# Shared threshold rows and a split of the column sums between GpSimd and VectorE, in a fused convolution and wavelet kernel

## The chip, the cores and the metric

The kernel runs on one core of a Trainium2 chip. The metric is the device time of one execution in microseconds (us). The core has five engines that this text names: TensorE (matmuls, "PE" in the profile, with its weight loads "PEld"), VectorE ("DVE"), ScalarE ("ACT"), GpSimd ("POOL") and SyncE ("SP"), which issues all the transfers of this kernel. Each engine works through its own list of instructions in the order in which the program gives them; semaphores make an instruction wait for one on another engine.

## The reference

The input x has 4 images of 64 channels of 256 x 256 float32 values. Four layers follow each other.

Layers 0, 2 and 3 are long convolutions. A small network with sines makes a filter along rows and one along columns for each channel; their outer product is convolved with the image (in the reference by FFT), and `x * bias` is added. Because the filter is an outer product, the kernel multiplies with a Toeplitz matrix along rows and with another along columns.

Layer 1 is a wavelet layer:

```python
f1 = haar2d(x)
for i in range(2):
    f3 = f1 * v[i]
    f4 = jnp.einsum('bchw,oc->bohw', f3, conv_w[i])
    f5 = jnp.sign(f4) * relu(jnp.abs(f4) - tau[i])
    acc = acc + f5
y = haar2d(acc, inverse=True) + x
```

The Haar transform along one axis takes sums and differences of neighbours, then again of the sums, for eight levels. `tau` is the threshold: one 256 x 256 map for each of the two branches, the same for all channels and images.

## The kernel before

**Phases.** Phase A does layer 0 and the forward Haar transform and stores coefficients in DRAM. Phase B multiplies by v, mixes channels with matmuls, takes the threshold (`less`, L680, and `threshold`, L685) and stores the mixed coefficients. Phase C does the inverse transform and layers 2 and 3. The images form two groups; phase B of the first group runs beside the second half of phase A, and phase B of the second group beside phase C.

**Phase A.** It has 64 rounds (`total`, L462), each of two channels of two images, and each round has ten pieces (`piece`, L524). In pieces 0 to 3 of round t TensorE does the rows of round t (`rows`), in pieces 4 and 5 the second half of the Haar transform of round t-3 as matmuls (`product`), and in pieces 6 to 9 the columns of round t-1 (`columns`). The PSUM results are put away one piece later (`flush`): after two column pieces VectorE makes two residuals, `x * bias + ps` (`residual`, L503), so a round has four of them, two in piece 8 and two in piece 0 of the next round. They fill the tile `x1`.

**The forward column sums.** `forward_free` (L362) does the first half of the Haar transform, along the free axis of `x1`. For half = 128, 64, 32, 16, 8, 4, 2, 1 it takes the differences (into the tile `fw`) and the sums (into a tile `h<half>`, which has one buffer and is the input of the next level) of neighbours. An instruction of level `half` writes 8 x half elements for each of 128 partitions: 1024, 512, 256, 128, 64, 32, 16, 8. It is a generator: each step issues one instruction, 16 in all, on GpSimd. The steps for round t-2 are taken in round t (L535 and L536): three in each of pieces 0 to 3, two in each of pieces 4 and 5. `x1` and `fw` have two buffers.

**The thresholds.** Before phase B, `scale_thresholds` (L313) loads `tau` into SBUF and multiplies it with a factor for each level. `put_thresholds` (L321) then copies it to DRAM, 64 times, one copy for each channel, because a step of phase B needs 128 partitions (64 channels x 2 rows) that all hold the same two rows. This takes 64 transfers of 512 KB. The DRAM rows are padded by 128 elements. `load_v` (L588) reads the copies back for each step of phase B, 64 steps for each group.

**The order of work.** `beside` (L1002) merges two lists of pieces. Up to piece 4 + 4 of round 34 it merges phase A with `rest` (L303): the networks of the other two layers, the copies of their filters, and the threshold writes, spread evenly (`merged`, L298). After that it merges phase A with phase B of the first group, whose units (`piece`, L722) have three pieces each: in the first VectorE multiplies (L663) and GpSimd adds (L703 to L707), in the second VectorE subtracts and applies the threshold (L683, L688) and TensorE mixes (L644). All transfers go through SyncE in program order.

Of the kernel before, what the change touches and what calls it, by code (L numbers as in the profile page):

```python
# [41 lines left out]
F32 = mybir.dt.float32  # L42
AF = mybir.ActivationFunctionType
ALU = mybir.AluOpType
# [3 lines left out]
P = 128  # L48
B, C, N = 4, 64, 256
# [9 lines left out]
ITEMS = 3  # L59
SPAN = ITEMS * PERIOD  # L60
REPEATS = 12
COPIES = 2 * REPEATS * ITEMS

FIRST = 4
# [35 lines left out]
def conv_haar_kernel(  # L100
# [13 lines left out]
    coef = [coefficients(f"coef{g}") for g in range(GROUPS)]  # L114
    mixed = [coefficients(f"mixed{g}") for g in range(GROUPS)]
    unshrunk = coefficients("unshrunk")
    thresholds = dram.tile([STEPS, 2, C, 2 * W + PAD], F32, tag="thresholds", name="thresholds")
    filt = [dram.tile([ROUNDS, 2, REPEATS, ITEMS, PERIOD], F32, tag=f"filt{l}", name=f"filt{l}") for l in range(NL)]

    def pool(name, bufs, stack=ctx, **kw):  # L120
# [174 lines left out]
    def half(r):  # L295
        return slice(r * ROW, (r + 1) * ROW)
# [16 lines left out]
    def scale_thresholds():  # L313

        per_level_sb = mp.tile([P, N], F32, tag="per_level", name="per_level_sb")
        nc.sync.dma_start(per_level_sb, per_level.partition_broadcast(P))
        nc.sync.dma_start(tau_sb.rearrange("p r w -> p (r w)"), tau)
        rows = tau_sb.rearrange("p r (h k) -> p (r h) k", k=N)
        nc.vector.tensor_tensor(rows, rows, per_level_sb.unsqueeze(1).to_broadcast([P, 4, N]), ALU.mult)

    def put_thresholds(copies, r, i):  # L321

        of = tau_sb[half(i), r].unsqueeze(1).to_broadcast([ROW, copies.stop - copies.start, W])
        nc.sync.dma_start(thresholds[:, r, copies, i * W : (i + 1) * W], of)

    puts = [(slice(n, n + 4), r, i) for n in range(0, C, 4) for r in range(2) for i in range(2)]
    rest = merged(rest, [scale_thresholds] + [lambda at=at: put_thresholds(*at) for at in puts])

    TILES = [(r, c) for r in range(2) for c in range(2)]

# [31 lines left out]
    def forward_free(src, dst, name):  # L362

        cur, half = src, HALF
        whole = dst.rearrange("p n (k q) -> p n k q", k=BLOCKS)
        to = dst.rearrange("p n (k q) -> p (n k) q", k=BLOCKS)
        while half > 0:
            sums = nxt = None
            if half > 1:
                nxt = ac.tile([P, 2 * M, half], F32, tag=f"h{half}", name=f"{name}{half}", bufs=1)  # L370
                sums = nxt
            else:
                sums = whole[:, :, 0:1, 0]
            if half < BLOCKS:
                pair = cur.rearrange("p n (t q) -> p n t q", q=2)
                diffs = whole[:, :, half : 2 * half, 0]
            else:
                m = half // BLOCKS
                pair = cur.rearrange("p n (k t q) -> p (n k) t q", k=BLOCKS, q=2)
                diffs = to[:, :, m : 2 * m]  # L380
                sums = sums.rearrange("p n (k t) -> p (n k) t", k=BLOCKS)
            even, odd = pair[:, :, :, 0], pair[:, :, :, 1]
            nc.gpsimd.tensor_tensor(diffs, even, odd, ALU.subtract)  # L383
            yield
            nc.gpsimd.tensor_tensor(sums, even, odd, ALU.add)
            yield
            cur = nxt
            half //= 2
# [70 lines left out]
    def phase_a():  # L459


        total = GROUPS * ROUNDS  # L462
        st = [dict() for _ in range(total)]

        def filters(t):
            if t < total:
                st[t]["toep"] = first_toep[t] if t < len(first_toep) else load_toeplitz(0, t)

        def load(t):
            if t < total:  # L470
                st[t]["x"] = first_x[t] if t < len(first_x) else load_x(t)

        def rows(t, j):
            s = st[t]
            if j == 0:
                s["y"] = big("t0", f"ay_{t}", 2)
            if j % 2 == 0:
                s["ps"] = banks(f"a1ps{j}_{t}")
            toeplitz(s["ps"], blocks(s["x"]), filters_x(s["toep"]), j)
            if j % 2:  # L480
                for r, ps in enumerate(s["ps"]):
                    y = blocks(s["y"])[:, r, j - 1 : j + 1]
                    later(lambda y=y, ps=ps: nc.scalar.copy(y, ps))  # L483

        def columns(t, j):
            s = st[t]
            if j == 0:
                s["x1"] = big("m0", f"x1_{t}", 2)
            if j % 2 == 0:
                s["ps2"] = banks(f"a2ps{j}_{t}")  # L490
            toeplitz(s["ps2"], blocks(s["y"]), filters_y(s["toep"]), j)
            if j % 2:
                for e, ps in enumerate(s["ps2"]):
                    later(lambda e=e, ps=ps: residual(t, e, j, ps))
            if j == BLOCKS - 1:
                s["fw"] = big("m1", f"fw_{t}", 2)
                s["ops"] = forward_free(s["x1"], s["fw"], f"f{t}_")

        def residual(t, e, j, ps):
            s = st[t]  # L500
            c = t % ROUNDS * CI + e
            to, old = (blocks(s[name])[:, e, j - 1 : j + 1] for name in ("x1", "x"))
            nc.vector.scalar_tensor_tensor(to, old, bias_sb[:, c : c + 1], ps, ALU.mult, ALU.add)  # L503

        def product(t, bp):
            s = st[t]
            if bp == 0:

                s["f"] = big("out", f"f_{t}", 2)
            two = banks(f"a3ps{bp}_{t}")  # L510
            fw = blocks(s["fw"])
            haar(two, lambda r, c: fw[half(r), c, 2 * bp : 2 * bp + 2], forward_sb)
            for b, ps in enumerate(two):
                f = s["f"][:, 4 * bp + 2 * b : 4 * bp + 2 * b + 2]
                later(lambda f=f, ps=ps: nc.scalar.copy(f, ps))  # L515

        def store(t):
            for to, f in all_rows(coef[t // ROUNDS], t % ROUNDS, st[t]["f"], t >= ROUNDS):
                nc.sync.dma_start(to, f)
            st[t].clear()  # L520

        middle = BLOCKS + 2

        def piece(t, j):  # L524
            flush()
            if t == 0 and j == 0:
                filters(0)
                filters(1)
                load(0)
                load(1)  # L530
            if j == 1 and t < 2:
                copies[t]()
            if j == 2:
                filters(t + 2)
            if j < middle and 1 < t:  # L535
                run(st[t - 2]["ops"], 3 if j < BLOCKS else 2)  # L536
            if j < BLOCKS:
                if t < total:
                    rows(t, j)
            elif j < middle:  # L540
                if 2 < t:
                    product(t - 3, j - BLOCKS)
            elif 0 < t <= total:
                columns(t - 1, j - middle)
            if j == middle + 1 and t > 2:
                store(t - 3)
            if j == A_PIECES - 1:
                load(t + 2)

        copies = spread(0, FIRST, ROUNDS, 2)  # L550
        pieces = [lambda t=t, j=j: piece(t, j) for t in range(total) for j in range(A_PIECES)]

        last = [lambda: [piece(total, j) for j in range(BLOCKS + 1)]]
        last += [lambda j=j: piece(total, j) for j in range(BLOCKS + 1, A_PIECES)]
        last += [lambda bp=bp: (flush(), product(total - 2, bp)) for bp in range(2)]
        t = total - 1
        end = [lambda: (flush(), run(st[t]["ops"], 16), store(t - 1))]
        end += [lambda bp=bp: (flush(), product(t, bp)) for bp in range(2)]
        end.append(lambda: (flush(), store(t)))
        return pieces, last, end  # L560

    def phase_b(grp):
# [25 lines left out]
        def load_v(s):  # L588
            if s >= STEPS:
                return  # L590
            d = st[s]
            d["v"], d["tau"] = [], []

            def fetch(first, count, tag):
                t = bp.tile([P, 2, count, W], F32, tag=tag, name=f"{tag}_{grp}_{first}_{s}", bufs=3)
                at = slice(first * W, (first + count) * W)
                nc.sync.dma_start(t[:, 0].rearrange("p i w -> p (i w)"), v[s, :, at])
                nc.sync.dma_start(t[:, 1].rearrange("p i w -> p (i w)"), thresholds[s].rearrange("r c w -> (r c) w")[:, at])
                d["v"] += [t[:, 0, i] for i in range(count)]
                d["tau"] += [t[:, 1, i] for i in range(count)]  # L600

            fetch(0, 2 if grp < GROUPS - 1 else 1, "v")
            if grp == GROUPS - 1 and not raw(2 * s + 1):
                fetch(1, 1, "raw")
# [564 lines left out]
```

## Time and profile before

| What | Value |
|---|---|
| Median of 3 runs | 2643.49 us (2638.67 to 2643.73) |
| The profiled execution | 2637.55 us, its span 2635.8 us |
| TensorE matmuls busy | 2323.6 us, 88% |
| VectorE busy | 1692.5 us, 64% |
| ScalarE busy | 1450.0 us, 55% |
| GpSimd busy | 2075.0 us, 79% |
| Transfers | 713.20 MB, 78.5% of the 16 DMA engines' time for the main queue |

The span is the time from the first to the last instruction. A row of the groups names the source line, the engine, the operation, output and inputs by their names in the program, the shape and the count; then the busy time in us and the mean of one in ns; then the idle time of the engine ahead of it and what ended that. The waits name who waited for whom, with the total in us, the number of times and the longest. A line number L383 is line 383 of the kernel before.

### The profile page before, as it was taken

To read this page: it belongs to the slowest core of one execution; us is meant where nothing else is said; L and a number is where in the kernel's file an instruction comes from. 1 tells how busy PE (TensorE), PEld (TensorE's weight loads), DVE (VectorE), ACT (ScalarE), POOL (GpSimd) and SP (SyncE) were. 2 spreads that over 40 slices of the span, in tenths; PEclk is the share of its full clock that TensorE was granted. 3 is DMA by queue.
4 is the path that set the end of the run, shared out by engine and by line. 5 is a ranking of instruction groups with operands and counts; after the bars stand their busy time and mean duration, and the time that the engine had idled before them with its cause. 6 is when DMAs were issued, how large, how long until landed. Compare 5 with 4: busy or idle time off the path is not lost.

```text
span 2635.8 us, 119315 instructions
## 1 busy us (share of the span) xinstructions
PE 2323.6 (88%) x53298; PEld 1950.2 (74%) x53298; DVE 1692.5 (64%) x1815; ACT 1450.0 (55%) x2446; POOL 2075.0 (79%) x2428
## 2 busy tenths in 40 slices
PE   6988788867777777788799999999989999999999
PEld 4778777745455444565578777777779999999999
DVE  4321112277887888975676777777757777777763
ACT  1333232256766777745566666666656555555652
POOL 1776666688888999987877777767879999999991
PEclk8999899988998999988899999999999999999999
DMA  6888898869989999975798889889966666666653
GB/s 190 273 278 282 267 276 273 300 227 341 317 305 330 330 346 347 346 251 186 261 324 316 316 310 332 319 311 316 331 218 223 213 212 214 219 214 212 219 169 111
DMA packets 238073, 713.20 MB, mean 271 GB/s; under 512 B 32238, under 2 KB 33583, under 8 KB 233336
## 3 DMA queue, kind: packets, MB, share of 16 engines
q1 hardware_dynamic: 237560, 705.57, 78.5%
q8 instruction: 419, 6.86, 1.1%
q14 instruction: 94, 0.77, 0.1%
HBM read 428.16 MB, written 277.28 MB: 268 GB/s over the span
## 4 chain that ended last, share of the span: by engine, by line
PE 41%; DVE 4%; DMA 3%; ACT 2%; issue 2%; POOL 1%; SPq 1%; DVEq 0%; ACTq 0%; POOLq 0%
PE c2c L335 9%; PE c2r L335 9%; PE c1r L335 8%; PE c1c L335 8%; PE c0ps L347 4%; PE f L644 3%; DVE cy L919 1%; DVE m L688 1%; DMA toep<-filt 1%; DMA g<-mixed 1%; DVE x L683 1%; DVE x L663 1%; ACT g L401 0%; POOL i L424 0%; ACT x L678 0%
## 5 line engine op out<-in xcount | busy, mean ns | idle before, releaser
L424 POOL TENSOR_TENSOR i<-i,g 128x16 f32<-128x16 f32 x744 | 438.5, 610 | 27.2
L335 PEld LDWEIGHTS a2ps<-toep,ay 64*64 64x64 f32 x8192 | 343.4, 140 | 126.6 <-ACT f L515 84.4
L644 PE MATMUL f<-ft,mix 64*64 64x512 f32 x2048 | 313.3, 632 | 123.4 <-DVE x L663 104.7
L335 PE MATMUL a1ps<-toep,x 64*64 64x256 f32 (+3 forms) x8192 | 353.9, 313 | 67.1 <-DMA x<-in_x 48.0
L335 PEld LDWEIGHTS a1ps<-toep,x 64*64 64x64 f32 x8192 | 316.5, 141 | 129.2 <-issue 70.1
L335 PE MATMUL a2ps<-toep,ay 64*64 64x128 f32 (+3 forms) x8192 | 360.9, 312 | 51.5 <-ACT f L515 50.8
L503 DVE SCALAR_TENSOR_TENSOR x<-x,bias_sb,a2ps 128x512 f32<-128x512 f32 x256 | 179.4, 742 | 337.8 <-issue 148.1
L335 PEld LDWEIGHTS c2c<-toep,ch 64*64 64x64 f32 x8192 | 306.5, 134 | 48.0 <-issue 24.7
L335 PEld LDWEIGHTS c1c<-toep,ch 64*64 64x64 f32 x8192 | 308.1, 134 | 42.4 <-issue 19.0
L483 ACT COPY ay<-a1ps 128x512 f32<-128x512 f32 x256 | 137.3, 589 | 365.2 <-PE a1ps L335 364.6
L335 PEld LDWEIGHTS c1r<-toep,z 64*64 64x64 f32 x8192 | 300.0, 135 | 28.9 <-issue 13.4
L424 POOL TENSOR_TENSOR ci<-i,g 128x1024 f32<-128x1024 f32 x124 | 316.6, 2574 | 4.5
L335 PE MATMUL c1r<-toep,z 64*64 64x64 f32 (+3 forms) x8192 | 316.0, 299 | 3.5 <-ACT z L888 1.8
L335 PEld LDWEIGHTS c2r<-toep,cy 64*64 64x64 f32 x8192 | 296.5, 134 | 29.8 <-issue 19.1
L335 PE MATMUL c2c<-toep,ch 64*64 64x128 f32 (+3 forms) x8192 | 311.6, 298 | 6.3 <-issue 3.5
L335 PE MATMUL c2r<-toep,cy 64*64 64x192 f32 (+3 forms) x8192 | 313.8, 298 | 3.2 <-issue 3.2
L335 PE MATMUL c1c<-toep,ch 64*64 64x128 f32 (+3 forms) x8192 | 311.6, 298 | 5.1 <-ACT ch L900 2.6
L706 POOL TENSOR_TENSOR gt<-m,ft 128x512 f32<-128x512 f32 x128 | 163.4, 1277 | 179.7 <-DVE m L688 179.7
L900 ACT COPY ch<-c2r 128x512 f32<-128x512 f32 x256 | 137.3, 590 | 281.8 <-PE c2r L335 281.1
L669 ACT ACTIVATE m<-x 128x1024 f32<-128x1024 f32 x194 | 206.3, 1063 | 144.7 <-DVE x L663 108.1
L383 POOL TENSOR_TENSOR fw<-x 128x1024 f32<-128x1024 f32 x64 | 121.7, 1902 | 189.9 <-DVE x L503 187.6
L663 DVE TENSOR_TENSOR x<-f,v 128x1024 f32<-128x1024 f32 x192 | 233.6, 1216 | 57.1 <-PE f L644 56.5
(85 smaller groups left out, 3983.6 us busy)
## 6 DMA issues: line engine op xcount, KB each, us to landing
toep<-filt SPq DMA_DIRECT2D x768, 112.0 KB
ft<-coef SPq DMA_DIRECT2D x128, 512.0 KB
mixed<-gt SPq DMA_DIRECT2D x128, 512.0 KB
g<-mixed SPq DMA_DIRECT2D x256, 256.0 KB
x<-in_x SPq DMA_DIRECT2D x128, 256.0 KB
thresholds<-tau_sb SPq DMA_DIRECT2D x64, 512.0 KB
coef<-f SPq DMA_DIRECT2D x128, 256.0 KB
x<-in_x SPq DMA_DIRECT2D x32, 1024.0 KB
```

The costliest lines, as they stand in the source:

```text
L335: nc.tensor.matmul(ps[r][half(c), j % 2, k * ROW :], data[half(r), c, k, bass.ts(j, ROW)], t(r, c)[:, : N - k * ROW], start=k == 0, stop=k ...
L347: nc.tensor.matmul(ps[r][half(c)].rearrange("p h k -> p (h k)"), matrix[half(r)], pairs(r, c).rearrange("p h k -> p (h k)"), start=True, s ...
L383: nc.gpsimd.tensor_tensor(diffs, even, odd, ALU.subtract)
L424: engine.tensor_tensor(to, s, d, op)
L483: later(lambda y=y, ps=ps: nc.scalar.copy(y, ps))
L503: nc.vector.scalar_tensor_tensor(to, old, bias_sb[:, c : c + 1], ps, ALU.mult, ALU.add)
L644: nc.tensor.matmul(un[u]["f4"][half(q), b, :], mixers[0][half(r), bass.ts(i, C)], st[s]["f"][half(r), b], start=True, stop=True, tile_posi ...
L663: nc.vector.tensor_tensor(un[u]["x"], un[u]["f4"], both(u, "v"), ALU.mult)
L669: nc.scalar.activation(un[u]["m"], un[u]["x"], AF.Sign)
L683: nc.vector.tensor_tensor(un[u]["a"], un[u]["a"], both(u, "tau"), ALU.subtract)
L706: nc.gpsimd.tensor_tensor(g[:, 0], m[:, 0], st[s]["f"][:, 0], ALU.add)
L900: later(lambda y=y, ps=ps: nc.scalar.copy(y, ps))
```

## The change

There are two edits.

**Thresholds.** The DRAM tile holds 16 copies of each row (`SHARED`) in place of 64. They are written by eight transfers, each with two copies of the whole scaled `tau` from all 128 partitions (1 MB), in place of 64 transfers of 512 KB. A load for phase B reads each copy into four neighbouring partitions; the number and the size of the loads stay. The layout of `tau` in SBUF changes with it (host side). Since the list of pieces is shorter, the multiplication moves from the first place of `rest` to one eighteenth of its length.

**Column sums.** The levels half = 8, 4, 2 and 1 (`COARSE`), eight instructions of 64, 32, 16 and 8 elements for each partition, are issued on VectorE in place of GpSimd. The steps are taken two in each of pieces 0 to 3 (the fine levels, on GpSimd) and two in each of pieces 6 to 9 (the coarse ones, on VectorE), none in pieces 4 and 5. They come after the piece's `flush`, so after the residuals in piece 8.

```diff
+SHARED = 16
+COARSE = 8
...
-    thresholds = dram.tile([STEPS, 2, C, 2 * W + PAD], F32, tag="thresholds", name="thresholds")
+    thresholds = dram.tile([STEPS, 2, SHARED, 2 * W + PAD], F32, tag="thresholds", name="thresholds")
...
-    def put_thresholds(copies, r, i):
-
-        of = tau_sb[half(i), r].unsqueeze(1).to_broadcast([ROW, copies.stop - copies.start, W])
-        nc.sync.dma_start(thresholds[:, r, copies, i * W : (i + 1) * W], of)
-
-    puts = [(slice(n, n + 4), r, i) for n in range(0, C, 4) for r in range(2) for i in range(2)]
-    rest = merged(rest, [scale_thresholds] + [lambda at=at: put_thresholds(*at) for at in puts])
+    def put_thresholds(copies):
+
+        n = copies.stop - copies.start
+        of = tau_sb.rearrange("p i w -> p (i w)").unsqueeze(1).to_broadcast([P, n, 2 * W])
+        nc.sync.dma_start(thresholds.rearrange("s r c w -> (s r) c w")[:, copies, : 2 * W], of)
+
+    rest = merged(rest, [scale_thresholds] + [lambda n=n: put_thresholds(slice(n, n + 2)) for n in range(0, SHARED, 2)])
...
-            nc.gpsimd.tensor_tensor(diffs, even, odd, ALU.subtract)
+            engine = nc.gpsimd if half > COARSE else nc.vector
+            engine.tensor_tensor(diffs, even, odd, ALU.subtract)
             yield
-            nc.gpsimd.tensor_tensor(sums, even, odd, ALU.add)
+            engine.tensor_tensor(sums, even, odd, ALU.add)
             yield
...
-            if j < middle and 1 < t:
-                run(st[t - 2]["ops"], 3 if j < BLOCKS else 2)
+            if not BLOCKS <= j < middle and 1 < t:
+                run(st[t - 2]["ops"], 2)
...
-                nc.sync.dma_start(t[:, 1].rearrange("p i w -> p (i w)"), thresholds[s].rearrange("r c w -> (r c) w")[:, at])
+                of = thresholds[s].rearrange("r c w -> (r c) w")[:, at].unsqueeze(1).to_broadcast([2 * SHARED, C // SHARED, count * W])
+                nc.sync.dma_start(t[:, 1].rearrange("p i w -> p (i w)"), of)
...
-        "tau": f(by_row("tau").transpose(2, 0, 1, 3).reshape(P, 2 * W)),
+        "tau": f(by_row("tau").reshape(P, 2 * W)),
```

More of the change, by code (lines that the diff above doesn't have):

```diff
@@ L316, in scale_thresholds @@
         nc.sync.dma_start(per_level_sb, per_level.partition_broadcast(P))
-        nc.sync.dma_start(tau_sb.rearrange("p r w -> p (r w)"), tau)
-        rows = tau_sb.rearrange("p r (h k) -> p (r h) k", k=N)
+        nc.sync.dma_start(tau_sb.rearrange("p i w -> p (i w)"), tau)
+        rows = tau_sb.rearrange("p i (h k) -> p (i h) k", k=N)
         nc.vector.tensor_tensor(rows, rows, per_level_sb.unsqueeze(1).to_broadcast([P, 4, N]), ALU.mult)
-    def put_thresholds(copies, r, i):
-        of = tau_sb[half(i), r].unsqueeze(1).to_broadcast([ROW, copies.stop - copies.start, W])
-        nc.sync.dma_start(thresholds[:, r, copies, i * W : (i + 1) * W], of)
-    puts = [(slice(n, n + 4), r, i) for n in range(0, C, 4) for r in range(2) for i in range(2)]
-    rest = merged(rest, [scale_thresholds] + [lambda at=at: put_thresholds(*at) for at in puts])
+    def put_thresholds(copies):
[3 more added lines that the diff above has]
+    rest = merged(rest, [scale_thresholds] + [lambda n=n: put_thresholds(slice(n, n + 2)) for n in range(0, SHARED, 2)])
     TILES = [(r, c) for r in range(2) for c in range(2)]
```

## The prediction

> **What bounds the kernel now.** The first view is the time by stage. Its columns: stretch in us, its length, then busy us and instruction count of TensorE (matmuls, weight loads), VectorE, ScalarE and GpSimd, the granted clock, the share of the 16 DMA engines, GB/s.
>
> ```profile
> 169.40:509.10 339.70, 287.21 (x6572) 262.75 (x6576) 67.49 (x96) 98.69 (x192) 227.27 (x385) 0.93 0.87 275
> ...
> 612.50:859.50 247.00, 186.87 (x3124) 128.61 (x3120) 204.68 (x191) 171.56 (x231) 213.80 (x235) 0.92 0.92 318
> 859.50:1132.20 272.70, 213.05 (x3748) 138.24 (x3744) 244.38 (x229) 206.69 (x277) 257.06 (x283) 0.97 0.96 340
> ```
>
> Row one is phase A beside the threshold writes ("stage 1"): VectorE idles for 80% of it, the transfers are at 87%. The others are phase A beside phase B's first group ("stage 2"): VectorE 83 and 90%, GpSimd 87 and 94%. From 1290 us on neither half of the change has work except the threshold reads.
>
> The waits of the first 600 us (total, times, longest):
>
> ```profile
> POOL fw L383 <- DVE x L503: 182.5, 33, 52.4
> ...
> PE a1ps L335 <- DMA x<-in_x: 48.0, 34, 3.5
> ```
>
> TensorE is late for the x loads, about once a round; GpSimd has time to spare. A round's length comes from the starts of the 1024-element column-sum pairs (L383): 54.4, 169.4 after nine rounds, 509.1 after 24 more, so 12.8 and 14.15 us. Single rounds of 10.4 us occur, so TensorE can do that.
>
> The groups by shape give the prices (busy us, mean ns):
>
> ```profile
> L383 POOL TENSOR_TENSOR fw<-x 128x1024 f32<-128x1024 f32 x64 | 121.7, 1902 | 189.9 <-DVE x L503 187.6 <-issue 2.2
> ...
> L383 POOL TENSOR_TENSOR fw<-f 128x64 f32<-128x64 f32 x64 | 18.8, 294 | 5.0
> ```
>
> The timelines (start, us) show how a round's parts follow each other in stage 1, and what a small VectorE operation meets while GpSimd runs:
>
> ```profile
> 320.47 1.41 DVE L503 SCALAR_TENSOR_TENSOR x<-x,bias_sb,a2ps 128x512 f32<-128x512 f32 x2 [0.72 <-PE a2ps L335]
> ```
>
> ```profile
> 321.96 1.89 POOL L383 TENSOR_TENSOR fw<-x 128x1024 f32<-128x1024 f32 x1 [0.69 <-DVE x L503]
> ```
>
> ```profile
> 1163.48 1.89 POOL L385 TENSOR_TENSOR f<-x 128x1024 f32<-128x1024 f32 x1
> 1163.64 1.84 DVE L426 SCALAR_TENSOR_TENSOR i_x<-g 128x8 f32<-128x8 f32 x2 [2.27 <-DMA g<-mixed]
> ```
>
> GpSimd's chain for a round starts 0.08 us after its last residual pair. The two 8-element operations at 1163.64 take 1.84 us: they end when the GpSimd operation does (1165.37), plus 0.1. Elsewhere the line takes 160 to 168 ns.
>
> A stage 2 round (residuals end at 927.6; its GpSimd chain starts there):
>
> ```profile
> 937.45 0.41 POOL L385 TENSOR_TENSOR f<-f 128x128 f32<-128x128 f32 x1
> ...
> 940.16 1.23 DVE L683 TENSOR_TENSOR a<-a,v 128x1024 f32<-128x1024 f32 x1 [1.06 <-ACT a L678]
> ...
> 943.77 1.40 DVE L503 SCALAR_TENSOR_TENSOR x<-x,bias_sb,a2ps 128x512 f32<-128x512 f32 x2
> ...
> 948.70 1.40 DVE L503 SCALAR_TENSOR_TENSOR x<-x,bias_sb,a2ps 128x512 f32<-128x512 f32 x2
> ```
>
> Level 16 is done at +10.3 us; VectorE stands still until +12.6 at piece 6; residuals at +16.2 and +21.1; the round ends at +22.5.
>
> [...] here the granted clock is 0.92 from 612 to 859 us and 0.97 after, and the rows don't show what starts the low spells. [...]
>
> **The threshold writes.** 64 issues of 512 KB (33.5 MB) become 8 of 1 MB (8.4 MB). Stage 1 moves 275 GB/s at 87%, so 316 at 100%: 25.2 MB less is 80 us of all 16 engines, 2.4 us a round over 33 rounds. SyncE saves 56 issues of 628 ns (median), 35 us or 1 us a round, off the path. Transfers then need about 12.2 - 2.4 = 9.8 us a round, TensorE 10.4. The reads keep count and size, but four neighbouring partitions read one row. The trace has no such pair to compare; 130 reads carry some 50 MB, 150 us of transfers at 340 GB/s, and 5% either way bounds it at ±7 us. I take 0: the Toeplitz loads also read shared copies. The multiplication of the thresholds moves from the start to after piece 0 of round 2. Two loads go before it on SyncE's queue, behind x; its VectorE wait (22.6 us now, at the start) has some 7 us of cover, while GpSimd sums round 0. If that cover were gone it would cost once, under 10 us.
>
> **The coarse levels in stage 1.** Eight GpSimd operations leave: 294+298+251+250+228+228+222+208 = 1.98 us. VectorE gains eight. [...] Two of one level overlap by about 0.08 us as those of L426 do, so the levels cost 0.40, 0.33, 0.29, 0.27 with their dependences, 1.3 us.
>
> The order matters more. Program order on VectorE in round t is: residuals of t-2 (piece 0), coarse 8 and 4 of t-2 (pieces 6, 7), residuals of t-1 (piece 8), coarse 2, coarse 1, residuals of t-1 (next piece 0). Coarse 8 waits for GpSimd's fine levels of t-2; behind it stand the residuals of t-1, and GpSimd's fine levels of t-1 wait for those. So a round holds one closed loop: fine levels 2(1.90+1.05+0.61+0.40) = 7.95, handing over 0.08, coarse 1.3, residuals 2 x 1.41, handing over 0.08: 12.25 us. GpSimd is idle during the VectorE part[...]. TensorE waits for banks that the residuals release, but has 1.9 us of room. The loop is longer than TensorE's 10.4 and the transfers' 9.8, and is the new bound: 12.3 to 12.6. Against 14.15 that is 24 x 1.7 = 40 us less; in the first nine rounds (12.8) the networks' VectorE work sits in the same queue, and I take no gain. Stage 1: **-40**.
>
> **The coarse levels in stage 2.** The merge puts 404 phase B pieces over 270 of phase A (L1002), so a round of ten holds five units of three. New GpSimd order: fine 128 and 64, add, fine 32 and 16, add, add. Level 16 still ends at +10.3. VectorE reaches piece 6 at +11.5 and idles to +12.6; GpSimd is then in an add (1.28 or 2.37 us each), so coarse 8 goes at its end, +11.7 to +12.75: delay 0 to 0.35. Coarse 4 at +15.1 waits for an add that ends near +15.3: 0.45 with its own time. Coarse 2 (+18.1) and coarse 1 (+20.9) find GpSimd between adds: 0.29 and 0.27. Sum 1.0 to 1.4 a round; 12 rounds x 1.2 = 14. In the ten rounds of 612 to 859 VectorE waits 2 to 4 us a round for TensorE at piece 7 (28.8 us for L663 in the waits of 600 to 850), which covers coarse 8 and 4: 10 x 0.6 = 6. Four opening rounds: 2. If the cover is gone, 0.7 more each. What is behind these waits: phase B's subtractions, then ScalarE's magnitudes and TensorE's mixing. GpSimd's 2 us less is worth nothing while VectorE leads. Stage 2: **+22**. Bounds: -10 (GpSimd's load was half the limit) and +80[...].
>
> **The end of phase A.** The last round's sums run in one stretch: 9.9 us on GpSimd become 8.0 + 1.4, but the coarse waits hold phase C's first residuals, which already wait 7.2 us for the same chain. **+3**.
>
> Sum: -40 + 22 + 3 = -15 from the profiled 2637.55 (span 2635.8 and 1.75 around it): 2622. The median, 2643.49, lies 5.9 higher: **2628**.
>
> **Rivals.**
> 1. [...] Each coarse pair in stage 2 that finds GpSimd entering an add first pays 1.28 or 2.37 more, 1.65 on average. For: the second of two 64-element operations of L426 lost its turn (649 ns). Against: at 1163.64 the pair passed together. One and a half lost pairs a round is 22 x 2.5 = 55: 2683. It decides from 0.7 us a round on (15/22): slower than before.
> 2. *TensorE's clock stays low through all of stage 2*[...]: 12 rounds at 25.6 instead of 23.9, +20: 2648.
> 3. *The writes did not set stage 1's pace* (bursts of x and coefficients do, so the loads stay late): -10 instead of -40: 2658.
> 4. *GpSimd was the limit in stage 2* (94% busy): its rounds get no longer, 2 us of them shorter by a little: -40 - 5 + 3: 2601.
>
> **How the numbers follow.** Main case 0.46 (its own range 2612 to 2638); rival 1: 0.22; rival 2: 0.10; rival 3: 0.09; rival 4: 0.13. Cases of both signs hold most of the chance. 0.2% is 5.3 us, about what a measurement of this kernel can tell from no change: faster is below 2638.2. Main (nearly all) and rival 4: 0.57; same, edges of main and half of rival 2: 0.09; slower 0.34. The range 2590 to 2685 leaves out the lower end of rival 4 and the upper half of rival 1, 0.2.
>
> **What would show it.** Stage 1 rounds near 12.4 with DMA near 0.75 and the x wait gone; GpSimd's 1024-element pair waiting for residuals, the residuals directly behind coarse operations that waited for GpSimd. Stage 2 rounds of 23.7 to 24 after 860 us, 25.5 before; coarse operations of 160 to 400 ns at pieces 8 and 9. Wrong if stage 1 rounds stay near 14 or reach 11, or if coarse operations of stage 2 average over 0.6 us.

## The result and the profile after

The changed kernel takes 2610.71 us, the median of 4 runs (2607.75 to 2618.91), against 2641.28 for the kernel before in the same comparison: a ratio of 0.989, 95% interval 0.986 to 0.992. It is 1.1% faster; the forecast was 2628 us. In the medians the change gives -31 us, twice the -15 of the forecast's sum. The profiled execution of the changed kernel took 2618.91 us (span 2616.8) and is the slowest of the four, so the -19 of its trace, below, looks closer to the forecast than the medians are.

The stretches below come from the starts of the rounds' 1024-element column sums (rounds 9, 33, 37, 47 and 59) and from the first `c2c` matmul of phase C, in the two profiled executions.

| Stretch | Before, us | After, us | Difference | Forecast |
|---|---|---|---|---|
| start to round 9 | 169.4 | 171.9 | +2.5 | 0 |
| rounds 9 to 33 (stage 1) | 339.7 | 284.2 | -55.5 | -40 |
| rounds 33 to 37 | 103.4 | 105.6 | +2.2 | +2 |
| rounds 37 to 47 (stage 2) | 247.0 | 252.4 | +5.4 | +6 |
| rounds 47 to 59 (stage 2) | 272.7 | 284.9 | +12.2 | +14 |
| round 59 to phase C | 117.7 | 122.2 | +4.5 | +3 |
| the rest | 1385.9 | 1395.6 | +9.7 | 0 |
| span | 2635.8 | 2616.8 | -19.0 | -15 |

The last stretch has no edit in it except four partitions sharing each threshold row. It is 1385.8 us in a kernel that shares rows in the same way (run e7 below) and 1388.8 in one that shares none (e4), and 1379.5 (e3) to 1393.3 us (e6) in the traces of all other runs. So I take the 9.7 for this one execution's own; what made it longer is not shown.

The time by stage of the changed kernel, its columns as in the prediction; the first row is rounds 9 to 33, the second rounds 47 to 59:

```profile
171.90:456.10 284.20, 269.96 (x6490) 239.01 (x6485) 88.94 (x288) 98.57 (x192) 185.28 (x193) 1.00 0.77 262
...
814.10:1099.00 284.90, 217.76 (x3748) 137.93 (x3744) 275.98 (x325) 205.46 (x277) 237.64 (x186) 0.96 0.93 325
```

In stage 1 the transfers fell from 87 to 77%, in a shorter time. In stage 2 VectorE is now busy for 275.98 of 284.90 us (97%, before 90%) and GpSimd for 83% (before 94%). The waits of the changed kernel up to 470 us (total, times, longest):

```profile
DVE fw L386 <- POOL f L388: 257.4, 33, 8.1
...
PE a1ps L337 <- DMA x<-in_x: 4.8, 5, 2.9
```

TensorE's wait for x is nearly gone (48.0 us in the first 600 us before); its matmuls wait 13.5 us in these 470 us for the residuals, 2.0 at the longest. In its place VectorE stands 8.1 us in nearly every round, at the first coarse operation, until GpSimd is done. One round in the timeline of the changed kernel (start, us):

```profile
297.85 0.40 POOL L388 TENSOR_TENSOR f<-f 128x128 f32<-128x128 f32 x1
...
298.28 0.23 DVE L386 TENSOR_TENSOR fw<-f 128x64 f32<-128x64 f32 x1 [8.07 <-POOL f L388]
...
298.89 1.40 DVE L506 SCALAR_TENSOR_TENSOR x<-x,bias_sb,a2ps 128x512 f32<-128x512 f32 x2
...
300.65 1.40 DVE L506 SCALAR_TENSOR_TENSOR x<-x,bias_sb,a2ps 128x512 f32<-128x512 f32 x2
...
302.13 1.89 POOL L386 TENSOR_TENSOR fw<-x 128x1024 f32<-128x1024 f32 x1 [3.89 <-DVE x L506]
```

This is the loop of the prediction: GpSimd ends level 16 at 298.25, VectorE starts level 8 0.03 us later; levels 8 and 4 take until 298.89, the residuals that stood behind them until 300.20, levels 2 and 1 until 300.65, the last residuals until 302.05; GpSimd starts the next round's level 128 0.08 later, ends its level 16 at 310.09, and so on. The matmuls that fill the residuals' tile `a2ps` end at 296.98, and still the first residuals start at 298.89, behind the coarse operations that stand ahead of them in VectorE's list: in this round VectorE keeps to the order of the program. From round 8 to round 33 the rounds of the trace take 11.8 us each, 11.84 on average.

### The profile page after: what moved, and what is told of

The parts are those of the page before. It is cut to its first block, busy times and chain, and to the rows that moved or that the text cites. A ratio compares the mean times of both kernels' runs of the same rounds, so it can differ in the third digit from the quotient of the medians.

```text
span 2616.8 us, 119195 instructions
## 1 busy us (share of the span) xinstructions
PE 2321.5 (89%) x53298; PEld 1924.2 (74%) x53298; DVE 1793.5 (69%) x2327; ACT 1447.4 (55%) x2446; POOL 1956.9 (75%) x1916
## 4 chain that ended last, share of the span: by engine, by line
PE 44%; DVE 3%; DMA 2%; issue 1%; ACT 1%; POOL 1%; SPq 1%; DVEq 0%; ACTq 0%; POOLq 0%
PE c2c L337 10%; PE c2r L337 10%; PE c1r L337 9%; PE c1c L337 8%; PE c0ps L349 4%; PE f L648 4%; DVE m L692 1%; DVE cy L923 1%; DVE x L667 1%; DVE x L687 1%; DMA g<-mixed 0%; SPq L164 0%; POOL i L427 0%; DMA rows<-in_v_rows 0%; DMA toep<-filt 0%
## 5 line engine op out<-in xcount | busy, mean ns | idle before, releaser
L427 POOL TENSOR_TENSOR i<-i,g 128x16 f32<-128x16 f32 x744 | 431.1, 600 | 27.2
L337 PEld LDWEIGHTS a2ps<-toep,ay 64*64 64x64 f32 x8192 | 336.7, 140 | 122.9 <-ACT f L518 75.6
L337 PE MATMUL a2ps<-toep,ay 64*64 64x256 f32 (+3 forms) x8192 | 358.6, 311 | 42.9 <-ACT f L518 42.4
L337 PEld LDWEIGHTS a1ps<-toep,x 64*64 64x64 f32 x8192 | 305.3, 138 | 96.4 <-issue 41.0
L337 PE MATMUL a1ps<-toep,x 64*64 64x192 f32 (+3 forms) x8192 | 353.5, 308 | 24.7 <-DVE x L506 13.5
L337 PE MATMUL c2c<-toep,ch 64*64 64x128 f32 (+3 forms) x8192 | 313.1, 299 | 11.6 <-ACT ch L904 11.2
L337 PE MATMUL c1r<-toep,z 64*64 64x192 f32 (+3 forms) x8192 | 315.4, 299 | 3.1 <-ACT z L892 1.8
L337 PE MATMUL c1c<-toep,ch 64*64 64x192 f32 (+3 forms) x8192 | 311.0, 297 | 5.7 <-issue 3.9
L386 DVE TENSOR_TENSOR fw<-f 128x64 f32<-128x64 f32 (+3 forms) x256 | 80.5, 314 | 289.7 <-POOL f L388 287.3
```

Of the source, the lines that this page charges most:

```text
L337: nc.tensor.matmul(ps[r][half(c), j % 2, k * ROW :], data[half(r), c, k, bass.ts(j, ROW)], t(r, c)[:, : N - k * ROW], start=k == 0, stop=k ...
L386: engine.tensor_tensor(diffs, even, odd, ALU.subtract)
L427: engine.tensor_tensor(to, s, d, op)
```

## The two edits apart

**Thresholds only (e1).** All sixteen column sums stay on GpSimd in their old places; the threshold writes and reads are those of the change.

```diff
-            engine = nc.gpsimd if half > COARSE else nc.vector
+            engine = nc.gpsimd
-            if not BLOCKS <= j < middle and 1 < t:
-                run(st[t - 2]["ops"], 2)
+            if j < middle and 1 < t:
+                run(st[t - 2]["ops"], 3 if j < BLOCKS else 2)
```

> The threshold edit alone; all sixteen column sums on GpSimd in their old places. Loop theory: nothing closes a loop any more, since no residual stands behind a wait for GpSimd; stage 1 falls to what TensorE and the transfers need, 10.5 to 11.0 us a round (24 x 1.0 less than the changed kernel's 11.84), and stage 2 goes back to 22.7 and 24.9, 17 less. Total 2560 to 2575. Rival, the loop only coincides with a limit of the transfers: stage 1 stays at 11.8, total about 2590. Rival, the coarse levels had to leave GpSimd for the writes to pay: stage 1 at 12.5 or more, total over 2605.

Measured: 2551.39 us (2544.00 to 2553.86), ratio 0.966 (0.963 to 0.969). Rounds 9 to 33 of this kernel:

```profile
159.60:417.50 257.90, 254.06 (x6535) 220.26 (x6530) 67.50 (x96) 98.74 (x192) 226.78 (x384) 1.00 0.84 290
```

Stage 1 takes 10.75 us a round and TensorE is busy for 254.06 of 257.90 us: without the loop it is TensorE that leads. Rounds 37 to 47 and 47 to 59 take 248.1 and 272.6 us, as before the change. So the loop theory holds and both rivals fall: the transfers allow 10.75 at the new size, and GpSimd needs no relief. The total is 9 us under the expected 2560 to 2575, most of it from the rounds before round 9, which starts 12.3 us earlier than with the change; I had counted only rounds 9 to 33 and stage 2.

**Coarse levels only (e2).** Thresholds written 64 times as before; the column sums as in the change.

```diff
-            nc.gpsimd.tensor_tensor(diffs, even, odd, ALU.subtract)
+            engine = nc.gpsimd if half > COARSE else nc.vector
+            engine.tensor_tensor(diffs, even, odd, ALU.subtract)
...
-            if j < middle and 1 < t:
-                run(st[t - 2]["ops"], 3 if j < BLOCKS else 2)
+            if not BLOCKS <= j < middle and 1 < t:
+                run(st[t - 2]["ops"], 2)
```

> The coarse levels on VectorE alone; thresholds written 64 times as before. Loop theory: the transfers set stage 1 as before (13.9 to 14.2 us a round), stage 2 is 1.0 longer a round in its later part and 0.5 in its earlier part: 2660 to 2670. Rival, the gain came from the column sums and not from the writes: 2610 to 2625.

Measured: 2666.94 us (2662.92 to 2672.55), ratio 1.010 (1.007 to 1.014). Stage 1 takes 14.09 us a round (338.2 in 24), as the kernel before; the loop of 11.84 is hidden under the transfers. Rounds 47 to 59 take 285.1 us in place of 272.7.

Alone the edits are worth -87 (2638.3 to 2551.4) and +29 us; together they give -31. The loop is enough for the missing 27 us: it costs nothing while transfers take 14.1 us a round, and 24 x (11.84 - 10.75) = 26 us in stage 1 once they don't. That 26 and 27 agree so closely is luck. By the traces the rounds before round 9 add another 11.5 us (round 9 starts at 171.9 with both edits, at 159.6 and 170.2 with one, at 169.4 with none), and the four profiled executions lie between 4 us under and 8 us over their medians.

## The loop

**Two levels only (e3).** The changed kernel with levels 8 and 4 back on GpSimd, in the same pieces. Now the wait for GpSimd stands at coarse 2, behind the first residual pair.

```diff
-COARSE = 8
+COARSE = 2
```

> The changed kernel with COARSE = 2: only levels 2 and 1 on VectorE, levels 8 and 4 on GpSimd. Loop theory: fine and middle levels 9.0 on GpSimd, then 0.45 of coarse sums and only one residual pair of 1.40 behind the wait, 0.1 of handing over: 11.0 us a round in stage 1 in place of 11.84, 20 less; stage 2 0.4 to 0.5 less a round, 10 less. Total 2575 to 2588. Rival, stage 1 is bound by something else at 11.84: total 2598 to 2606.

Measured: 2569.43 us (2567.50 to 2578.08), ratio 0.974 (0.970 to 0.978), under the expected total. Stage 1 takes 267.3 us for 24 rounds, 11.14 each. The timeline of this kernel:

```profile
308.09 0.24 POOL L388 TENSOR_TENSOR f<-f 128x32 f32<-128x32 f32 x1
...
308.36 0.18 DVE L386 TENSOR_TENSOR fw<-f 128x16 f32<-128x16 f32 x1
...
309.07 1.41 DVE L506 SCALAR_TENSOR_TENSOR x<-x,bias_sb,a2ps 128x512 f32<-128x512 f32 x2 [0.17 <-PE a2ps L337]
...
310.56 1.89 POOL L386 TENSOR_TENSOR fw<-x 128x1024 f32<-128x1024 f32 x1 [2.23 <-DVE x L506]
```

GpSimd's part grew from 7.96 to 9.09 us (299.24 to 308.33), VectorE's behind it fell to 0.55 of sums and one residual pair of 1.41; with 0.03 and 0.08 of handing over that is 11.16 us, and most rounds take 11.1. The round shown takes 11.3, because the last residuals wait 0.17 us for TensorE here: at 11.1 us GpSimd's loop and TensorE are nearly level. The stage moved by the amount that the loop's sum gives. The total fell more than I had expected (41 us, not 30): rounds 0 to 9 are 6.9 us shorter than with the change, the end of phase A 1.3, and phase C of this profile 16 us shorter than of the profile of the change, of which 9.7 had been that execution's own excess.

**Coarse levels behind the residuals (e5).** The same sixteen instructions on the same engines, but VectorE does the coarse ones of round t-3 in pieces 0 to 3 of round t, beside GpSimd's fine ones of round t-2.

```diff
-            if not BLOCKS <= j < middle and 1 < t:
-                run(st[t - 2]["ops"], 2)
+            if j < BLOCKS:
+                for k in (t - 3, t - 2):
+                    if k >= 0:
+                        run(st[k]["ops"], 2)
...
-        last += [lambda bp=bp: (flush(), product(total - 2, bp)) for bp in range(2)]
+        last += [lambda bp=bp: (flush(), run(st[total - 2]["ops"], 16), product(total - 2, bp)) for bp in range(2)]
```

> The changed kernel with the coarse levels a few pieces later: VectorE does those of round t-3 in pieces 0 to 3 of round t, behind both residual pairs, while GpSimd does the fine levels of round t-2. Same instructions on the same engines. Loop theory: residuals no longer stand behind a wait for GpSimd, so stage 1 falls from 11.84 to 10.5 to 11.3 us a round, 22 less. [...] now each coarse pair meets GpSimd in operations of 0.4 to 1.9 us, so in stage 2 it waits about 0.7 to 1 us a pair where it waited 0 to 0.35: 1.5 to 3 more a round than the changed kernel, 33 to 66 in 22 rounds. Total 2620 to 2655. Rival, the order does not matter: 2605 to 2615.

Measured: 2734.05 us (2732.58 to 2737.13), ratio 1.036 (1.034 to 1.037), far outside every expected total: stage 1 is not shorter but 13.67 us a round. In the 22 rounds of stage 2 the 33 to 66 us expected for pairs that meet GpSimd came at their lower end, 573.2 us in place of 537.3. The timeline of this kernel in stage 1, and a wait of TensorE from 170 to 440 us:

```profile
302.29 1.95 POOL L386 TENSOR_TENSOR fw<-x 128x1024 f32<-128x1024 f32 x1 [4.98 <-DVE x L506]
302.52 1.79 DVE L386 TENSOR_TENSOR fw<-f 128x32 f32<-128x32 f32 x1
...
304.21 1.95 POOL L388 TENSOR_TENSOR f<-x 128x1024 f32<-128x1024 f32 x1
...
304.43 1.77 DVE L386 TENSOR_TENSOR fw<-f 128x16 f32<-128x16 f32 x1
```

```profile
PE a3ps L349 <- DVE fw L388: 45.4, 20, 2.5
```

A 32-element subtraction that takes 0.22 us in the changed kernel's stage 1 (217 ns on average up to 509 us) takes 1.79 here: it ends at 304.31, the 1024-element operation beside it at 304.24. Level 2 then waits behind the next one (1.77) and level 1 behind the third (0.99), so the coarse sums last 5.2 us in place of 1.06, and TensorE's `product` of that round, a few pieces on, waits for them. I had priced the waits only for stage 2 and had not asked who waits for the coarse sums when they move. So this run doesn't test the loop; it shows what coarse operations cost when they run beside GpSimd's long ones, 5.2 us a round. That the wait of `product` is all that lengthens stage 1 is not shown.

## The threshold writes

**64 copies, wide (e4).** The changed kernel with the old number of copies, written in the new shape: 32 transfers of 1 MB from 128 partitions.

```diff
-SHARED = 16
+SHARED = 64
```

> The changed kernel with SHARED = 64: again 33.5 MB of thresholds, but in 32 transfers of 1 MB from 128 partitions, and every partition of a load reads a row of its own. Theory: the transfers need 9.0 us of the 11.84 us a round (share 0.76); 25.2 MB more at 346 GB/s adds 2.2, 11.2 in all, which is still under the loop's 11.84, so stage 1 is 11.9 to 12.3 a round and the total 2613 to 2625. Rival, bytes set the pace at any shape: 13.5 to 14 us a round, total 2650 to 2660. If sharing a row by four partitions cost or saved anything, the stretches after stage 1 differ by more than 5 us from the changed kernel's.

Measured: 2607.07 us (2604.09 to 2611.53), ratio 0.988 (0.985 to 0.991): no different from the changed kernel, and 6 us under the expected 2613. Its list of pieces is long enough that the multiplication of the thresholds stands early again (VectorE does it at 45.0 us, with the change at 58.96), and round 9 starts 5.0 us earlier. Stage 1 takes 11.98 us a round, at 318 GB/s and 89%. Behind the loop, 25.2 MB of writes cost 0.14 us a round. Rounds 33 to 59 take 641.2 us, with the change 642.9: rows shared by four partitions cost and save nothing.

**64 copies, wide, without the loop (e6).** The column sums of e1, so an edit of one number to that kernel.

```diff
-SHARED = 16
+SHARED = 64
```

> Column sums all on GpSimd in their old places, 64 copies of the thresholds, in 32 transfers of 1 MB from 128 partitions. With the loop gone, stage 1 shows what the bytes cost. If the old writes were slow by their bytes alone: 13.5 to 14 us a round, total 2625 to 2640. If they were slow by their shape (64 partitions, 2 KB rows) and the 128-partition ones run at the 346 GB/s worked out before, the transfers need 11.2 us a round: 11.2 to 11.7, total 2565 to 2580. With 16 copies it was 10.7 and 2551.

Measured: 2572.31 us (2569.48 to 2583.35), ratio 0.975 (0.973 to 0.977). Rounds 9 to 33 of this kernel:

```profile
152.60:445.30 292.70, 268.10 (x6533) 239.95 (x6529) 67.50 (x96) 98.92 (x192) 226.75 (x384) 0.98 0.89 317
```

12.2 us a round: the same bytes as before the change at 317 GB/s, where the kernel before moved 275 at about the same share of the engines. So of the 3.4 us between 14.15 and 10.75 some 1.95 are the shape of the writes (128 partitions with rows of 4 KB for 64 with rows of 2 KB, half as many transfers) and the rest their amount, as far as TensorE lets it show. Which of these properties of the shape does it was not tried. The round is longer than the 11.2 to 11.7 that I expected, and why is not shown; the total lies in its range partly because round 9 starts at 152.6 us, 7 us before that of e1, since the multiplication stands early here too (45.9 us).

**16 copies, narrow (e9).** 16 transfers of 512 KB, each from 64 partitions as before the change; otherwise as e7 below. The main line of its edit, against the kernel before:

```diff
-puts = [(slice(n, n + 4), r, i) for n in range(0, C, 4) for r in range(2) for i in range(2)]
+puts = [(slice(n, n + 4), r, i) for n in range(0, SHARED, 4) for r in range(2) for i in range(2)]
```

> 16 copies of the thresholds, but written as before from 64 partitions in rows of 2 KB: 16 transfers of 512 KB; the multiplication first, all column sums on GpSimd. Stage 1 has been 14.15 us a round with 64 narrow copies, 12.2 with 64 wide ones, 10.9 with 16 wide ones. If the narrow shape costs per transfer as it did there (1.95 us a round for 64), 16 narrow ones cost 0.5 a round more than 16 wide ones where transfers lead, and nothing where TensorE leads: 10.9 to 11.3, total 2540 to 2556. If the shape alone were the cause, it would be 12.5 or more and 2580.

Measured: 2542.80 us (2540.80 to 2547.18), ratio 0.965 (0.962 to 0.967). Stage 1 takes 10.96 us a round. With 16 copies the shape makes no difference that can be seen (e7: 10.91): TensorE leads, busy for 256.72 of 263.10 us.

**The multiplication first (e7).** e1 with the multiplication of the thresholds in the first place of the list again.

```diff
-    rest = merged(rest, [scale_thresholds] + [lambda n=n: put_thresholds(slice(n, n + 2)) for n in range(0, SHARED, 2)])
+    rest = [scale_thresholds] + merged(rest, [lambda n=n: put_thresholds(slice(n, n + 2)) for n in range(0, SHARED, 2)])
```

> The threshold edit alone (all column sums on GpSimd), with the multiplication of the thresholds back at the first place of the list. Now VectorE waits 13.7 us for it at 45 to 59 us, in a round with residuals behind it, and the first two rounds take until 70 us. Theory: 3 to 6 us less than the threshold edit alone, 2545 to 2549. Rival: the wait is covered, no difference (2550 to 2553).

Measured: 2542.21 us (2541.19 to 2547.89), ratio 0.963 (0.961 to 0.964), beside 0.966 (0.963 to 0.969) for e1 in another comparison, so the intervals touch. The traces agree on the place: round 9 starts at 153.5 us in place of 159.6. The total is 3 us under the expected 2545. With e9, from which it can't be told apart, it is the fastest version that was run, and faster than both kernels.

**8 copies (e8).** e7 with half as many copies, each read by eight partitions.

```diff
-SHARED = 16
+SHARED = 8
```

> As the kernel with the multiplication first, with 8 copies of each row in four transfers, each read by eight partitions. Theory: TensorE sets stage 1 now (10.4 to 10.7), so 4 MB less bring 0 to 4 us, and sharing a row by eight costs nothing: 2541 to 2549. Rival, sharing costs: stages with threshold reads get longer by over 5 us.

Measured: 2588.63 us (2586.26 to 2593.93), ratio 0.981 (0.979 to 0.982): 46 us over e7, by the rival and more. Stage 1 is as short as expected (10.58 us a round); rounds 37 to 47 and 47 to 59 take 260.8 and 303.3 us in place of 247.1 and 272.5. The second of these rows and a wait of phase B from 506 to 1070 us:

```profile
767.30:1070.60 303.30, 223.04 (x3748) 139.75 (x3744) 245.64 (x229) 206.39 (x277) 256.68 (x282) 0.92 0.98 307
```

```profile
DVE x L667 <- DMA v<-in_v: 53.3, 25, 5.3
```

The DMA engines are busy for 98% and move 307 GB/s; e7 moves 342 at 97% in those rounds. VectorE waits 53.3 us for phase B's inputs, in e7 0.4. Rows shared by four partitions are free here (342 GB/s at 97% in e7, 340 at 96% before the change), by eight they are not. Whether that comes from eight reads of one row or from only 16 rows serving 128 partitions was not told apart.

## Why the prediction was right

**The loop** was right in its parts and its order, and its sum a little high: 12.25 us forecast (the terms as printed add up to 12.2), 11.84 measured. GpSimd's fine levels took 7.96 (7.95 forecast). The coarse levels took 0.61 and 0.45, 1.06 in all, in place of 1.3, and the residuals 1.31 and 1.40, in place of 2.82, since most of these instructions start about 0.1 us before the one ahead of them ends (in the round shown, level 8's sums start at 298.42 and its differences end at 298.51). I then took 12.3 to 12.6 for disturbances; there were none, because the loop left room for all others. That is the mis-sized term of the sum: stage 1 gave -55.5 and not -40, which is most of the 17 us between forecast and median. The transfers' need was sized too high as well, 9.8 us a round forecast and 0.77 x 11.84 = 9.1 measured: I counted the bytes that go and not the shape, which e6 shows to matter. Behind the loop that had no effect.

**The price of a coarse operation.** The forecast's 0.40, 0.33, 0.29 and 0.27 us a level were the author's estimate. The trace of before has these of L426 on VectorE (count, then ns: least, median, most):

```profile
L426 DVE SCALAR_TENSOR_TENSOR i_x<-g x4: 160/168/1759, 1163.6 to 1177.0; 128x8 f32<-128x8 f32 x4
...
L426 DVE SCALAR_TENSOR_TENSOR ci<-g,i_m x4: 1220/1227/2922, 1173.3 to 1189.9; 128x1024 f32<-128x1024 f32 x4
```

A straight line through the two medians gives an estimate of 226, 193, 176 and 168 ns for 64 to 8 elements. The pairs' means up to 509 us, where GpSimd is mostly idle, come within 13% of it: 231 and 249, 217 and 184, 180 and 168, 171 and 165.

**Stage 2** gave +1.02 us a round after round 47 (1.0 to 1.4 forecast) and +0.54 before (0.6). The place within the round was not quite as I had it. From 600 to 1130 us, the changed kernel's groups on VectorE:

```profile
L386 DVE TENSOR_TENSOR fw<-f 128x64 f32<-128x64 f32 x22 | 27.9, 1270 | 8.7 <-POOL f L388 8.7
L388 DVE TENSOR_TENSOR f<-f 128x64 f32<-128x64 f32 x22 | 23.4, 1062 | 0.0
```

In the round whose sums start at 909.07:

```profile
919.33 2.36 POOL L707 TENSOR_TENSOR gt<-gt,m 128x1024 f32<-128x1024 f32 x1
...
919.84 1.94 DVE L386 TENSOR_TENSOR fw<-f 128x64 f32<-128x64 f32 x1
...
921.63 1.29 POOL L710 TENSOR_TENSOR gt<-m,ft 128x512 f32<-128x512 f32 x1
...
921.69 1.33 DVE L388 TENSOR_TENSOR f<-f 128x64 f32<-128x64 f32 x1
...
922.93 1.24 DVE L687 TENSOR_TENSOR a<-a,v 128x1024 f32<-128x1024 f32 x1
```

Both operations of level 8 last until a GpSimd addition ends, one after the other, 1.94 and 1.33 us (231 and 249 ns on average up to 509 us), where I had let the pair pass together. It costs more than the 0 to 0.35 us that I gave it: phase B's subtraction follows at +13.9 and not at +12.6. Level 4 is cheap instead (206 and 184 ns, where I had counted 0.45 us with a wait), since no GpSimd addition is running when it comes, 925.34 us in this round. As at 1163.64 before the change, where the small pair ended 0.1 us after GpSimd's operation, each of the two ends about 0.1 us after the addition beside it (921.78 after 921.69, 923.02 after 922.92).

**The moved multiplication** is where the forecast was too kind: it stands at nothing in the sum, with some 7 us of cover, and at under 10 us if the cover were gone.

```profile
58.96 1.23 DVE L321 TENSOR_TENSOR tau_sb<-tau_sb,per_level_sb 128x1024 f32<-128x1024 f32 x1 [13.67 <-DMA tau_sb<-in_tau]
```

VectorE waits 13.67 us for its load, which SyncE issues at 52.33 us, behind x (from 49.17), and the coarse sums and residuals of the first rounds stand behind it. Round 9 starts 2.5 us later than before, though round 0 starts 9 us earlier. e1 and e7, which differ in this place alone, put the price at 6.1 us (round 9 at 159.6 and 153.5), inside the bound.

**The rivals.** Rival 1 (a coarse pair that meets a GpSimd addition pays for it) held for level 8 alone, 1270 and 1062 ns, where idle time covered most of it: in rounds 47 to 59 VectorE is busy for 31.6 us more, but its idle time falls from 28.3 to 8.9 us and the stretch grows by 12.2. e5 shows the price where more of the pairs meet GpSimd. Rival 2 (a low clock) did not come: 0.96 and 0.91, before 0.97 and 0.92; what sets the clock is not shown. Rival 3 is excluded by e1 and e2. Rival 4 is excluded by e1: without GpSimd's relief rounds 37 to 59 take 520.7 us, with it 537.3 (519.7 before the change).

**What I did not see** is the size of what the second edit costs beside the first: 59 us (2551.39 to 2610.71). The numbers for it stood in the prediction, 12.25 for the loop against 10.4 for TensorE and 9.8 for the transfers, but I set the loop only against the old 14.15.

## What to carry to other kernels

When work moves to an engine, write down what stands behind its first wait in the engine's list (here residuals ran only behind coarse operations that had waited 8.07 us) and whether the engine waited for needs one of those things: if so, the two engines take turns, and the sum of their turns is a lower bound of the round that no utilisation of the two shows (here GpSimd was busy for 65% of stage 1 and VectorE for 31%). Judge each edit of a combined change against the limit that the other edit leaves, not against the old one. Relief is worth something only for an engine that leads: GpSimd, busy for 94% of rounds 47 to 59, did not.

## What the runs showed that I had not expected

- Threshold loads whose DRAM rows are each read by four partitions (32 rows) cost nothing; with eight partitions to a row (16 rows) they are slower, 307 GB/s at 98% in place of 342 at 97%. Which of the two numbers does it is open.
- The same 33.5 MB of writes, in 32 transfers from 128 partitions with 4 KB rows in place of 64 from 64 partitions with 2 KB rows, make the rounds of stage 1 1.95 us shorter (14.15 and 12.2, one trace each).
- A 32-element subtraction on VectorE beside 1024-element GpSimd operations takes 1.79 us in stage 1 (e5), in place of 0.22.
